# Layer 1's entry in a four-layer graph network: the first norm's statistics taken where z is made, the second norm applied by ScalarE

## The chip, the cores and the metric

The kernel runs on one core of a Trainium2 chip. Its time is the device time of one execution in microseconds (us). Five engines of the core work side by side, each on its own instructions in a fixed order: TensorE (PE, with its weight loads as PEld) multiplies matrices into PSUM, VectorE (DVE) and ScalarE (ACT) work on rows, GpSimd (POOL) does small side work here, and SyncE (SP) issues the loads and stores (DMAs). An instruction waits until what it reads is there, and those behind it on its engine wait with it. All data are 32-bit floats.

## The reference, cut to what matters

Four layers on 3327 nodes with 256 features each, all of the form `x = x + layer(relu(layernorm(x)))`. The change concerns the seam between layer 0 and layer 1:

```python
# layer 0, in two steps n: A is an attention with the smallest probabilities cut off, R the normalised adjacency
Xf = R @ Xf ; Xa = A @ Xa ; Z = Z + Xf @ U1[n].T + Xa @ U2[n].T
h = X + Z                                        # "z" below
x = x + (h - mean(h)) / sqrt(var(h) + 1e-5) * ln_g + ln_b      # the first norm
# layer 1's entry
h = maximum(layernorm(x), 0)                     # the second norm
h2 = tanh(h @ W_proj + b_proj)
gw = h2 @ W_gcn
# layer 1's products
feat = relu(filtered_adj @ gw + b_gcn) ; x = x + feat
```

So for each node row z is normalised, scaled and added to x, and the new x is normalised once more before two small products. Layers 2 and 3 are graph attentions and are not touched.

## The kernel before, in words

The 3327 rows are padded to 26 tiles of 128 rows, and a tile of rows has the nodes on the partitions. The function layer0 (inside layers) holds layer 0 and layer 1's entry.

Step 2 of layer 0 goes over the tiles in groups of three; the last group, the ninth, has two (tiles 24 and 25). For a group, the function group makes logits (line 1037), moves them out of PSUM (1011), takes exponentials (1020), and searches for the threshold of each row in four rounds. A round counts mass with long passes over 3328 columns, on ScalarE (1121, two passes per tile) or on VectorE (1126), and ends in a chain of some 14 VectorE operations on one or two columns (1132 to 1153). After the last round each tile has three more long VectorE passes (1168, 1171, 1182). Then the generator weighted transposes the tile's weights through PSUM (950, 952), multiplies them with the features (940), transposes two rows of results (785, 786), multiplies by U1 and U2 (970) and adds the base row: line 978 makes zrow, a buffer of one, which line 979 stores to zz_d in DRAM. The generator neighbours runs the other product (914) beside it.

Layer 1's entry is the generator entered, in turns divided by yield. Turn 1 loads the row of x (1263) and z back from DRAM (1267) and calls norm_of on z: bn_stats and bn_aggr on VectorE (131, 132) and two one-column GpSimd operations (792, 793: add epsilon, power of minus one half). Turn 2 applies the first norm on VectorE in two passes (1270, 1271) and calls norm_of on the new x. Turn 3 applies the second norm on VectorE (scaled_by, 797), transposes on TensorE (785) and copies out of PSUM with a relu on ScalarE (786). Turns 4 and 5 are the two products (1280, 1285 and 1291, 1294). The buffers of z form a ring of six, inside the slot called kt, which layer 1 uses later for pos_first (1490).

The order of the work comes from two places. The function overlapped steps all running generators once per tick: entries start one per tick, in the last group's rounds (tile it at tick 160 + 12 + it, tiles 24 and 25 at tick 208), and within a tick the older entries come first and the groups last. Then a scheduler that works when the program is built turns this sequence into one fixed order for each engine: an instruction that it finds ready may go ahead of an earlier one that it finds waiting. The trace shows such moves: line 1271 of tile 0 runs after a pass of line 1126 that the sequence has before it, and the loads of x run in two blocks of 13 and 14.

After the entries come weights for layers 2 and 3 (1329 to 1335), and layer 1: per tile of rows it loads a block of the transposed adjacency (1469), filters it (1472, 1473) and multiplies it with gw (1476), while adjacency rows (1488) are turned into masks (1490) and stored (1494). Layer 2's entry (the class Entry) already has the form in which ScalarE applies the norm: its stats adds a third GpSimd operation that forms minus mean times scale (1388), and tile_in has one activation with that bias and scale (1394).

Of the kernel before, what the change touches and what calls it, by code (L numbers as in the profile page):

```python
# [9 lines left out]
F32 = mybir.dt.float32  # L10
# [4 lines left out]
AF = mybir.ActivationFunctionType  # L15
# [5 lines left out]
P = 128  # L21
# [45 lines left out]
def kernel(  # L67
# [678 lines left out]
    def layers(fast):  # L746
# [34 lines left out]
        def transposed(src, dst, relu=False):  # L781

            ps = ps_row()
            for c in range(2):
                nc.tensor.transpose(ps[:, c * P : (c + 1) * P], src[:, c * P : (c + 1) * P], ident)
            nc.scalar.activation(dst, ps[:, :D], AF.Relu if relu else AF.Copy)

        def norm_of(src, pool, name):

            mv = pool.tile([P, 2], F32, tag=name, bufs=3, name=name)  # L790
            stats_of(mv, src)
            nc.gpsimd.tensor_scalar(mv[:, 1:2], mv[:, 1:2], EPS, None, ALU.add)
            nc.gpsimd.tensor_tensor(mv[:, 1:2], mv[:, 1:2], minus_half, ALU.pow)  # L793
            return mv

        def scaled_by(dst, src, mv):
            nc.vector.tensor_scalar(dst, src, mv[:, 0:1], mv[:, 1:2], ALU.subtract, ALU.mult)


        def layer0(wp, mp, ap_, tp, sp):  # L800
# [125 lines left out]
            def weighted(s, it, e, norm, xa, xa_next, us):  # L926

                if s == 0:
                    base = h(it)[:, :D]
                else:  # L930
                    base = tp.tile([P, D], F32, tag="base", bufs=1, name="base_row")
                    nc.sync.dma_start(base, zz_d[it * P : (it + 1) * P, :])
                xf_in = tp.tile([P, D], F32, tag="xf_in", name="xf_in")
                nc.sync.dma_start(xf_in, (xf_d, xf2_d)[s][it * P : (it + 1) * P, :])
                po = ps_out0()[:, :D]

                def products(wt, j0, m):
                    for k in range(m):
                        jc = j0 + k
                        nc.tensor.matmul(  # L940
                            po, wt[:, k * P : (k + 1) * P], xa(jc)[:, :D], start=(jc == 0), stop=(jc == NT - 1)
                        )

                ready = None
                for j0 in range(0, NT, 8):
                    m = min(8, NT - j0)
                    pt = ps_wide()
                    for k in range(m):
                        jc = j0 + k
                        nc.tensor.transpose(pt[:, k * P : (k + 1) * P], e[:, jc * P : (jc + 1) * P], ident)  # L950
                    wt = tp.tile([P, 8 * P], F32, tag="wt", name="wt")
                    nc.scalar.copy(wt[:, : m * P], pt[:, : m * P])  # L952
                    if ready:
                        products(*ready)
                    ready = wt, j0, m
                    yield
                products(*ready)
                if s == 0:
                    row = xa_next(it)[:, :D]
                else:  # L960
                    row = tp.tile([P, D], F32, tag="xa_row", bufs=1, name="xa_row")
                nc.scalar.mul(row, po, norm)
                yield
                xt = turned(row, "xt", 2)
                xft = turned(xf_in, "xft", 2)
                yield
                pz = ps_row()
                for n, (lhs, u) in enumerate(((xft, us[0]), (xt, us[1]))):
                    for cc in range(2):
                        nc.tensor.matmul(  # L970
                            pz[:, :D], lhs[:, cc, :], u[:, cc, :],
                            start=(n == 0 and cc == 0), stop=(n == 1 and cc == 1),
                        )
                if s == 0:
                    keys_of(xt, 1, it)
                yield
                zrow = tp.tile([P, D], F32, tag="zrow", bufs=1, name="zrow")
                nc.vector.tensor_tensor(zrow, pz[:, :D], base, ALU.add)
                nc.sync.dma_start(zz_d[it * P : (it + 1) * P, :], zrow)
                yield  # L980
                if s == 0:

                    xb = tp.tile([P, D], F32, tag="xa_row", bufs=1, name="xb")
                    r = rows_of(it)
                    for a, b in rows_to_load(it):
                        nc.sync.dma_start(xb[a:b], x[it * P + a : it * P + b])
                    nc.gpsimd.tensor_tensor(xb[:r], xb[:r], b_b[:r], ALU.add)
                    nc.sync.dma_start(xb_d[it * P : it * P + r, :], xb[:r])


            b_b = tp.tile([P, D], F32, tag="base", bufs=1, name="b_b")
            nc.sync.dma_start(b_b, bass.AP(tensor=ln_b.tensor, offset=ln_b.offset, ap=[[0, P], [1, D]]))
# [267 lines left out]
            def entered(it):  # L1260
                wps, wgs, g_b, bp, xs_, gw_, temps = places()
                for a, b in rows_to_load(it):
                    nc.sync.dma_start(xs_(it)[a:b], xb_d[it * P + a : it * P + b])

                hz, ht = temps[:, it % 6], temps[:, 6 + it % 2]
                h2 = hz
                nc.sync.dma_start(hz, zz_d[it * P : (it + 1) * P, :])
                mv = norm_of(hz, sp, "mv_z")
                yield
                nc.vector.scalar_tensor_tensor(hz, hz, mv[:, 0:1], g_b, ALU.subtract, ALU.mult)  # L1270
                nc.vector.scalar_tensor_tensor(xs_(it), hz, mv[:, 1:2], xs_(it), ALU.mult, ALU.add)
                mv = norm_of(xs_(it), sp, "mv_1")
                yield
                scaled_by(hz, xs_(it), mv)
                transposed(hz, ht, relu=True)
                yield
                ps = ps_row()
                for m in range(2):
                    for c in range(2):
                        nc.tensor.matmul(  # L1280
                            ps[:, m * P : (m + 1) * P], wps[:, c, m * P : (m + 1) * P],
                            ht[:, c * P : (c + 1) * P], start=(c == 0), stop=(c == 1),
                        )
                for m in range(2):
                    nc.scalar.activation(
                        h2[:, m * P : (m + 1) * P], ps[:, m * P : (m + 1) * P], AF.Tanh, bias=bp[:, m : m + 1]
                    )
                yield
                ps = ps_acc()
                for c in range(2):  # L1290
                    nc.tensor.matmul(
                        ps[:, :D], h2[:, c * P : (c + 1) * P], wgs[:, c, :], start=(c == 0), stop=(c == 1)
                    )
                nc.scalar.copy(gw_(it), ps[:, :D])
                yield
# [433 lines left out]
```

## Time and profile before

| | us |
|---|---|
| median of three runs (lowest, highest) | 3117.26 (3114.98, 3118.21) |
| profiled execution | 3111.67 |
| its span, first to last instruction | 3109.9 |
| PE, DVE, ACT, POOL busy in the span | 2831.8, 2382.5, 1968.2, 375.5 |
| step 2 of layer 0, until the last group's logits | 1065 to 1813 |
| entries of layer 1 (lines 1267 to 1294) | 1814.8 to 2018.9 |
| layer 1's products | 1998 to 2352 |

Stretches are counted in us from the start of the span. Busy time is the time in which an engine ran instructions of the program; matmuls are pipelined and their ends are modelled, so a busy PE is near its limit but not proven to be at it. A wait is put down to the instruction that released it. "Idle before" an instruction is time in which its engine stood still. The view of the chain that ended last follows from the last instruction back to what released each step.

### The profile page before, as it was taken

The numbers are of one execution on the slowest core, as the hardware profiler recorded it, in microseconds if no ns is written. First come the engines' busy times: TensorE is split into PE (matmuls) and PEld (weight loads), VectorE is DVE, ScalarE is ACT, GpSimd is POOL, SyncE is SP. The second block draws the span as 40 slices with busy tenths as digits, with TensorE's granted clock in tenths as the row PEclk, the third lists the DMA queues.
The fourth block names the chain that finished last, engine by engine and source line by source line (L and its number), as shares of the span: only waits on it lengthen the run. The fifth ranks groups of instructions, "written<-read, shape, count | busy, mean of one in ns | idle before, by whom it ended". The sixth has DMA issues, their size and how long they took to land. (4 is left out here: it accounts for less than half of the span.)

```text
span 3109.9 us, 37662 instructions
## 1 busy us (share of the span) xinstructions
PE 2831.8 (91%) x13454; PEld 2278.7 (73%) x13454; DVE 2382.5 (77%) x4159; ACT 1968.2 (63%) x2607; POOL 375.5 (12%) x716
## 2 busy tenths in 40 slices
PE   7788899999999899999999988999997999979998
PEld 5466677777778577767777767788876787758887
DVE  3678888778873588888976868577765999769996
ACT  6767787768763666677665645333334776757776
POOL 0220010000001000000000014311120233210000
PEclk9899999999999999999999999999998999989999
DMA  4431112331242232211232232388861211112221
GB/s 137 131 102 51 55 42 77 91 89 49 70 119 88 76 97 60 59 43 51 73 89 79 76 110 75 111 315 313 321 228 33 71 59 57 31 49 78 72 76 38
DMA packets 183034, 298.83 MB, mean 96 GB/s; under 512 B 24700, under 2 KB 137015, under 8 KB 179511
## 3 DMA queue, kind: packets, MB, share of 16 engines
q1 hardware_dynamic: 182838, 296.34, 30.3%
q8 instruction: 108, 1.77, 0.2%
q14 instruction: 88, 0.72, 0.1%
HBM read 251.97 MB, written 44.30 MB: 95 GB/s over the span
## 5 line engine op out<-in xcount | busy, mean ns | idle before, releaser
L1121 ACT ACTIVATE junk_a<-e,minus 128x3328 int8<-128x3328 f32 x208 | 638.7, 3071 | 3.7
L1588 PE MATMUL ps_wide<-wh,places 128*128 128x257 f32 x1872 | 452.5, 384 | 35.9 <-DVE places L1582 34.8
L1588 PEld LDWEIGHTS ps_wide<-wh,places 128*128 128x128 f32 x1872 | 354.4, 192 | 94.5 <-ACT places L1580 16.5
L914 PE MATMUL ps_acc<-h,blk 128*128 128x258 f32 x1352 | 333.6, 399 | 44.5 <-ACT xf_row L922 35.3
L1011 DVE TENSOR_SCALAR_CACHE_REDUCE e<-ps_wide 128x1024 f32<-128x1024 f32 (+1 forms) x176 | 178.4, 1019 | 212.0 <-PE ps_wide L1037 211.5
L914 PEld LDWEIGHTS ps_acc<-h,blk 128*128 128x128 f32 x1352 | 262.1, 199 | 99.9 <-ACT xf_row L922 40.5
L914 PE MATMUL ps_acc<-xf,blk 128*128 128x256 f32 x1352 | 314.0, 384 | 13.0 <-ACT xf_row L922 13.0
L940 PE MATMUL ps_out<-h,wt 128*128 128x256 f32 x1352 | 312.6, 383 | 5.0 <-ACT wt L952 4.9
L940 PE MATMUL ps_out<-xa,wt 128*128 128x256 f32 x1352 | 312.6, 381 | 1.4 <-ACT wt L952 1.4
L1579 ACT ACTIVATE places<-places,sd 128x512 f32<-128x512 f32 (+1 forms) x364 | 246.6, 685 | 105.5 <-PE ps_wide L1588 72.3
L1476 PE MATMUL ps_wide<-gw,blk 128*128 128x256 f32 x1352 | 303.9, 382 | 0.2 <-ACT blk L1473 0.2
L914 PEld LDWEIGHTS ps_acc<-xf,blk 128*128 128x128 f32 x1352 | 254.1, 191 | 63.2 <-ACT xf_row L922 18.5
L1476 PEld LDWEIGHTS ps_wide<-gw,blk 128*128 128x128 f32 x1352 | 257.0, 192 | 35.1 <-ACT blk L1473 0.6
L940 PEld LDWEIGHTS ps_out<-h,wt 128*128 128x128 f32 x1352 | 250.8, 191 | 41.1 <-ACT wt L952 7.0
L940 PEld LDWEIGHTS ps_out<-xa,wt 128*128 128x128 f32 x1352 | 248.3, 190 | 34.9 <-ACT wt L952 3.7
L1126 DVE SCALAR_TENSOR_TENSOR below<-e,v 128x3328 f32<-128x3328 f32 x72 | 265.4, 3687 | 1.8
L1580 ACT ACTIVATE places<-places,d 128x512 f32<-128x512 f32 (+1 forms) x364 | 235.9, 682 | 46.1 <-DVE places L1581 45.7
L1581 DVE TENSOR_TENSOR places<-places,places 128x1024 f32<-128x1024 f32 (+1 forms) x182 | 210.4, 1164 | 67.8 <-ACT places L1579 65.8
L952 ACT COPY wt<-ps_wide 128x1024 f32<-128x1024 f32 x208 | 175.1, 846 | 88.1 <-PE ps_wide L950 87.4
L1037 PE MATMUL ps_wide<-keys,q 64*128 64x512 f32 (+1 forms) x832 | 214.8, 567 | 16.0 <-DVE e L1011 13.1
L1582 DVE SCALAR_TENSOR_TENSOR places<-blk_s,places 128x1024 f32<-128x1024 int8 (+1 forms) x182 | 206.1, 1141 | 2.0
L1020 ACT ACTIVATE e<-e,nm 128x3327 f32<-128x3327 f32 x44 | 134.8, 3064 | 85.3 <-DVE nm L1019 85.2
(274 smaller groups left out, 4314.8 us busy)
## 6 DMA issues: line engine op xcount, KB each, us to landing
blk<-in_adj_t SPq DMA_DIRECT2D x104, 448.0 KB, 3.4
blk<-in_adj_t SPq DMA_DIRECT2D x52, 832.0 KB, 6.8
adj_rows<-in_adj SPq DMA_DIRECT2D x25, 1663.5 KB, 8.1
blk<-in_adj_t SPq DMA_DIRECT2D x104, 384.0 KB, 3.3
blk_s<-sign_d SPq DMA_DIRECT2D x72, 256.0 KB, 2.9
blk_s<-pos_d SPq DMA_DIRECT2D x44, 416.0 KB, 3.6
pos_d<-pos SPq DMA_DIRECT2D x22, 416.0 KB, 2.8
xf_d<-xf_row SPq DMA_DIRECT2D x52, 128.0 KB, 2.4
```

What stands on the lines that cost most here:

```text
L914: nc.tensor.matmul(acc[:, :w], blk[:, j, :], xf(jc)[:, :w], start=(jc == 0), stop=(jc == NT - 1))
L940: nc.tensor.matmul(po, wt[:, k * P : (k + 1) * P], xa(jc)[:, :D], start=(jc == 0), stop=(jc == NT - 1))
L1011: nc.vector.tensor_scalar(e.rearrange("p (f c) -> p f c", f=2)[:, :, c0 : c0 + cw], pl.rearrange("p (f c) -> p f c", f=2)[:, :, :cw], 1.0, ...
L1037: nc.tensor.matmul(pl[:, f * 512 : f * 512 + cw], q[f * DA : (f + 1) * DA, :], kt[f * DA : (f + 1) * DA, s, c0 : c0 + cw], start=True, sto ...
L1121: nc.scalar.activation(junk, es[i], (AF.Relu, AF.Sign)[n], bias=minus[:, 0, i : i + 1], accum_out=(ga, sa)[n][:, 0, i : i + 1],)
L1126: nc.vector.scalar_tensor_tensor(below, es[i], v[:, 3, i : i + 1], es[i], ALU.is_ge, ALU.mult, accum_out=v[:, 1, i : i + 1],)
L1476: nc.tensor.matmul(po, filt[:, j * P : (j + 1) * P], gw(jc), start=(jc == 0), stop=(jc == NT - 1))
L1579: nc.scalar.activation(e1[:, :, q, :], s0, AF.Exp, bias=sd[:, jc + q, 1:2])
L1580: nc.scalar.activation(e2[:, :, q, :], s1, AF.Exp, bias=d2[:, jc + q : jc + q + 1])
L1581: nc.vector.tensor_tensor(e1, e1, e2, ALU.max)
L1582: nc.vector.scalar_tensor_tensor(e1, signs[:, :n, j : j + 2, :], 0.0, e1, ALU.is_gt, ALU.min)
L1588: nc.tensor.matmul(pos_[k], e1[:, k, q, :], wh(jc + q)[:, : D + 1], start=(jc + q == 0), stop=(eye and jc + q == NT - 1),)
```

## The change

The statistics of z are computed in weighted, directly behind the line that makes zrow, for step 2 only, into a tile mv_z that holds mean and scale of all 26 tiles; turn 1 of entered then only issues the two loads, and turn 2 reads mv_z. The second norm is no longer applied by VectorE: GpSimd forms minus mean times scale in place of the mean, and a ScalarE activation computes relu(scale * x + bias) from SBUF into the buffer that is transposed; the copy out of PSUM behind the transposes becomes a plain copy. Nothing else differs.

```diff
-        def norm_of(src, pool, name):
-
-            mv = pool.tile([P, 2], F32, tag=name, bufs=3, name=name)
+        def norm_of(src, pool, name, mv=None):
+
+            if mv is None:
+                mv = pool.tile([P, 2], F32, tag=name, bufs=3, name=name)
             stats_of(mv, src)
...
                 nc.vector.tensor_tensor(zrow, pz[:, :D], base, ALU.add)
                 nc.sync.dma_start(zz_d[it * P : (it + 1) * P, :], zrow)
+                if s == 1:
+                    norm_of(zrow, sp, "mv_z", mv_z[:, it, :])
                 yield
...
+            mv_z = sp.tile([P, NT, 2], F32, bufs=1, name="mv_z")
...
                 nc.sync.dma_start(hz, zz_d[it * P : (it + 1) * P, :])
-                mv = norm_of(hz, sp, "mv_z")
                 yield
+                mv = mv_z[:, it, :]
                 nc.vector.scalar_tensor_tensor(hz, hz, mv[:, 0:1], g_b, ALU.subtract, ALU.mult)
                 nc.vector.scalar_tensor_tensor(xs_(it), hz, mv[:, 1:2], xs_(it), ALU.mult, ALU.add)
                 mv = norm_of(xs_(it), sp, "mv_1")
+                nc.gpsimd.tensor_scalar(mv[:, 0:1], mv[:, 0:1], mv[:, 1:2], -1.0, ALU.mult, ALU.mult)
                 yield
-                scaled_by(hz, xs_(it), mv)
-                transposed(hz, ht, relu=True)
+                nc.scalar.activation(hz, xs_(it), AF.Relu, bias=mv[:, 0:1], scale=mv[:, 1:2])
+                transposed(hz, ht)
                 yield
```

## The prediction

> **What bounds the kernel now.** The page's busy shares come first: PE 91%, DVE 77%, ACT 63%, POOL 12% of a span of 3109.9 us. TensorE bounds the kernel on average, but the changed lines work in one stretch only, so I looked for the place. The instructions of lines 1270 and 1271 run from 1822.9 to 2010.3 us, and those of line 978 for the second step from 1165.1 to 2002.2. The stretch table (columns: stretch, length, then busy us and instruction count of PE, PEld, DVE, ACT, POOL, granted clock, DMA share, GB/s) cuts this in five:
>
> ```profile
> 1065.00:1813.00 748.00, 702.71 (x3408) 550.38 (x3406) 589.74 (x1131) 503.70 (x460) 44.79 (x125) 1.00 0.25 70
> 1825.00:1838.60 13.60, 6.22 (x29) 5.13 (x27) 12.90 (x15) 6.89 (x6) 1.56 (x4) 0.91 0.77 235
> 1838.60:1977.00 138.40, 118.37 (x654) 98.92 (x655) 119.83 (x283) 68.87 (x132) 57.71 (x101) 0.95 0.20 67
> 1977.00:2002.20 25.20, 25.19 (x141) 22.51 (x142) 3.52 (x10) 7.92 (x18) 2.85 (x11) 1.00 0.25 84
> 2002.20:2020.40 18.20, 15.52 (x80) 12.95 (x79) 10.27 (x32) 5.67 (x10) 5.72 (x10) 1.00 0.67 220
> ```
>
> In the body of step 2 (first row) PE is busy 94%, DVE 79%: PE is the bound. In the 138.4 us of entries (third row) DVE is busy 119.8 us; the waits of DVE in that same window are these:
>
> ```profile
> DVE temps L797 <- POOL mv L793: 12.0, 22, 0.8
> DVE xs L1271 <- POOL mv_z L793: 6.1, 12, 0.7
> ```
>
> 119.8 + 18.1 = 137.9 of 138.4 us: DVE has no free time here, and all its waiting is for GpSimd's two short operations of a norm. PE idles 20.0 us of it (138.4 - 118.4). The chain that ended last says the same. One entry's turn, word for word:
>
> ```profile
> 1920.01 0.74 DVE bn_st L131 x2
> 1920.76 0.09 DVE mv L132
> 1920.85 0.08 issue
> 1920.93 0.23 POOL mv L792
> 1921.16 0.07 issue
> 1921.23 0.69 POOL mv L793
> 1921.92 0.21 POOL mv_z L792
> 1922.13 0.07 issue
> 1922.20 0.60 POOL mv_z L793
> 1922.82 0.49 DVE xs L1271
> ```
>
> The reader should see the loop DVE, POOL, POOL, DVE. Line 1271 starts at 1919.28, 1922.82, 1926.17 and 1929.60: 3.44 us per entry, in which DVE works about 2.5 and waits twice 0.46. Between these instructions lie the small operations of the last group's search (L1132, L1133, L1140, ...), one at a time, so the search is stretched too; its last product (line 1182 of tile 25) ends at 1962.5. From 1977 on PE is full (25.19 of 25.20). After 2020.4 layer 1's products are near PE's limit, with one DMA-fed chain beside them (adj_rows, pos, 1490), and start when the entries' buffer is released.
>
> **What the Trainium skill says.** (1) "SBUF — State Buffer", section "Who interferes with whom": a VectorE instruction with two SBUF inputs and a GpSimd instruction that reads SBUF exclude each other for the whole instruction. The trace agrees: a power on one column, 0.57 to 0.61 us as a rule, took 3.80 us beside such a pass:
>
> ```profile
> 1910.88 3.69 DVE L1126 SCALAR_TENSOR_TENSOR below<-e,v 128x3328 f32<-128x3328 f32 x1
> 1911.19 3.80 POOL L793 TENSOR_TENSOR mv<-mv,minus_half 128x1 f32<-128x1 f32 x1
> ```
>
> (2) "Perfetto Trace Analysis", section "Tensor Engine Instruction (MATMUL, LD_WEIGHTS)": ACT, DVE and GpSimd are strict first-in-first-out, so a waiting instruction holds all behind it. The two waits above agree: other DVE work was ready. (3) "ScalarE: Activation LUTs", section "What ACT_TABLE_LOAD costs": 186 ns, 0.833 ns per element and 93 ns per pointer operand, an estimate of 585 ns for 256 columns with both; the same form in layer 2's entry shows 600, so 0.60 us is used:
>
> ```profile
> L1394 ACT ACTIVATE hr<-xs,mv_a x52: 584/600/603, 2039.6 to 2748.5; 128x256 f32<-128x256 f32 x52
> ```
>
> Its section "Table sets: the hidden batching unit" says that relu is in every set; the trace has no table load after the first softmax, so none is added.
>
> **The change part by part.**
> *Statistics of z moved.* At the entry DVE loses one bn_stats (0.41), one bn_aggr (0.17), and the normalising pass of line 797 (0.41): 22.0 us by the groups of this window (8.9 + 4.0 + 9.1). Neighbouring DVE instructions overlap by about 0.08 us (bn_stats starts at 1920.35, the next starts at 1920.67), so 67 of them free about 22.0 - 5 = 17 us. The 18.1 us of waits go as well: line 1270 and 1271 now read values made long before, and nothing on DVE reads mv_1 any more. The pair put behind line 978 comes back as 0.58 us raw, about 0.5 effective; three of these zrows fall in the window (1.5 us). DVE then needs 119.8 - 17 + 1.5 = 104 us of 138.4. It stops being the bound; PE, with 118.4 us of work, is next. So at most 20.0 us is to be had here, and a PE with nothing else to change would have to be fed without a gap.
> *How much of the 20.0 us.* PE's idle in the window that the waits put on DVE is 8.8 us before L785 on an L1174 (most of it, 7.5 us, ending at 1838.7, before the window), 8.3 on L797, 3.9 on a bank held until line 978 ran, 1.7 on L132, the rest issue gaps and ACT. The L797 waits and most of the gaps shrink with the DVE chain; the 3.9 us sit behind long passes of 3.7 us (1168, 1182), which stay. I take 12 us of 20; the ends are 0 and 20.
> *Head of the stretch.* 7.4 us of PE idle at 1825 to 1838.6 are two long DVE passes in front of entry 0's first statistics. They stay: 0.
> *ScalarE's pass.* 26 x 0.60 = 15.6 us added; 22 of them, 13.2 us, in the window, where ACT has 68.9 us of work: 82.1 of 138.4. The copy out of PSUM stays at 0.38 us. Per entry the way from statistics to transposes grows by one GpSimd multiply (0.27, line 1388's row) and 0.19 us of pass, 0.5 us; entries are pipelined, so this is latency and costs nothing except at the last one. What is late if ACT waits: the copies of line 952 behind it, and so PE.
> *GpSimd.* The two operations on mv_z move, one multiply is added: 26 x 0.27 = 7 us on an engine with 80 us free in the window.
> *Body of step 2.* About 21 pairs, 21 x 0.5 = 10.5 us of DVE in 748 us where DVE has 158 us free and PE 45. They wait for nothing but line 978 before them. Cost 0, hidden by PE's products; if that cover were gone, 10.5 us. Their GpSimd operations stand before line 912's add on that queue; it is busy 44.8 of 748 us there, so 0, at most a few of the 3.8 us blocks.
> *DMAs.* None is added. The read of z on SP's queue keeps its place; the first DVE instruction to wait for it is now line 1270, a turn later. SP's queue itself is unaffected.
> *Buffers.* mv_z is kept for all tiles until line 1271 of the last one, 208 bytes per partition for three times 8. A later tile laid over it could start to load only then; w2l's load is issued at 2004.73 now, so this costs between 0 and the 2 to 3 us to that line; I take 0.
> *The last tile.* Its z lands at 2006.55. The pair and the GpSimd detour before line 1271 (9.85 - 6.55 = 3.3 us) shrink to 0.4: -2.9, and +0.5 for the longer second norm. But the first pass of line 1490 (2020.39) stands on DVE behind two loads of ab, 2005.73 and 2013.66 to 2019, whose only stretch by this chain is one 0.76 us wait among line 1335's first four. I count -1; ends 0 and -3.
> *Afterwards.* Layer 1 starts that much sooner and keeps its own length: what is won at 2020 is won at the end.
>
> Sum: -12 - 1 + 0 = -13 us. The profiled execution took 3111.67 us (span 3109.9, 1.8 around it); it would take 3098.7. The median shown, 3117.26, is 5.6 us above that execution: 3104.3, said as 3104.
>
> **Rivals.**
> *PE is fed without a gap:* all 20 us and 3 at the end: 3094. For it: DVE has 34 us to spare. Against: long passes stay where they are.
> *The gain stays hidden:* the order on each engine is fixed when the program is built, and the last group's search, not DVE's sum, sets the end: four rounds of two 3.07 us ACT passes and a chain of some 14 small DVE operations. If DVE's freed time turns into idle before that chain, about 2 us are left, 3115. For it: between 1825 and 1929 a round takes some 26 us, far above its own chain of about 10, so there is room to gain; that speaks against.
> *ScalarE becomes the bound (slower):* the new pass waits on ACT for GpSimd's column, which long two-input DVE passes block for 3.8 us. In layer 2's entry, the same form, ACT waited 59.9 us in 26 cases for line 1388, 2.3 us each. 22 x 2.3 = 50.6 us against 56.3 us free on ACT: nearly all its slack, with line 952's copies and the search's passes behind. It decides once more than 0.6 us per entry reaches PE beyond today's waits (22 x 0.6 = 13); at 1.0 us, 22 - 13 = +9: 3126. Against: there ACT had little else to do, and today's order already makes ACT wait 27.6 us for line 785.
>
> **How the numbers follow.** Forecast 0.48 (3098 to 3110), PE fed throughout 0.15, hidden 0.15, ScalarE the bound 0.22. Faster by over 0.2%, about 6 us and about what a measurement of this kernel can tell, 0.63; within it 0.15; slower 0.22. The range 3089 to 3125 takes in the full 20 us and most of the slower case; the forecast's own range is 3098 to 3110.
>
> **What would show it.** Right: in the stretch of entries, no DVE wait for GpSimd; line 1271 every 2 us or so where it was every 3.44; tile 25's line 1182 ends between 1942 and 1954, not at 1962.5; PE over 90% busy in it; line 1490 starts near 2007. Wrong: ACT waits on mv for tens of us with PE waiting for line 952; or the body of step 2 longer than before; or DVE idle in the stretch with the last search ending no sooner.

## The result, and the profile after

The changed kernel takes 3102.19 us (median of 6 runs, 3098.58 to 3106.23), the kernel before beside it 3116.12 us (6 runs, 3112.79 to 3121.76). The ratio is 0.9949, with a 95% interval of 0.9938 to 0.9961: faster, by 12 to 19 us. The profiled span went from 3109.9 to 3099.1 us.

That is the forecast's size. The traces show that it did not come from where the forecast put it. From here on line numbers are those of the changed kernel unless said otherwise: 793 and 794 are GpSimd's epsilon and power, 1275 and 1276 the two passes of the first norm (1270, 1271 before), 1278 GpSimd's new product, 1280 ScalarE's new pass, 1286 and 1297 the entry's two products with their evictions 1291 and 1300 (1280, 1291, 1285, 1294 before), 1478, 1482, 1492 and 1496 layer 1's filter, product, clearing and mask (1472, 1476, 1486, 1490 before).

Milestones of the two traces, in us from the start of the span:

| | before | after |
|---|---|---|
| last group's search done (last line 1153 of before) | 1929.06 | 1918.00 |
| first norm of the 24th entry | 1977.32 | 1963.19 |
| last zrow | 2002.20 | 2002.89 |
| last copy of an entry's second product | 2018.51 | 2019.06 |
| first mask of layer 1 | 2020.39 | 2018.89 |
| last product of layer 1 | 2351.45 | 2342.87 |
| from there to the end | 758.4 | 756.2 |

The search ends 11 us sooner, the first norms of 24 entries are done 14 us sooner, and yet the last entry leaves at the same time. The gain appears after that: layer 1's products take 324.0 us where they took 331.1.

The stretch table of the changed kernel (length, then busy us and count of PE, PEld, DVE, ACT, POOL, granted clock, DMA share, GB/s): body of step 2, stretch of entries, end of the entries, layer 1.

```profile
1065.00:1813.00 748.00, 702.70 (x3401) 549.97 (x3400) 597.43 (x1171) 503.83 (x460) 84.73 (x165) 0.99 0.25 70
1838.60:1977.00 138.40, 117.71 (x648) 104.68 (x649) 103.51 (x223) 79.47 (x154) 62.58 (x89) 0.89 0.21 70
1977.00:2018.90 41.90, 39.32 (x221) 34.60 (x219) 9.92 (x34) 13.58 (x31) 5.06 (x20) 1.00 0.42 143
2018.90:2343.00 324.10, 311.90 (x1460) 269.32 (x1461) 222.12 (x248) 107.91 (x147) 52.38 (x104) 1.00 0.78 287
```

In the second row VectorE fell from 119.8 to 103.5 busy us, as worked out (104). TensorE did not follow: 648 matmuls in 117.7 us, where before had 654 in 118.4. The waits of ScalarE, VectorE and TensorE in that same window, from three answers on waits (engine, its line, who released it: total us, times, longest):

```profile
ACT temps L1280 <- POOL mv L1278: 36.3, 13, 6.4
...
DVE temps L1275 <- DMA temps<-zz_d: 11.6, 5, 4.2
DVE temps L1275 <- PE ps_row L785: 6.4, 1, 6.4
...
PE ps_acc L1297 <- ACT temps L1291: 16.1, 6, 6.2
PE ps_row L785 <- ACT temps L1280: 10.0, 1, 10.0
```

VectorE waits for GpSimd no more, as forecast. ScalarE does, 36.3 us in this window and 44.7 us from 1840 to 2020, and TensorE waits 26.6 us for ScalarE (2.6 before). The longest of these waits, 10.0 us, began 6.0 us ahead of the window; the other 20.6 us are nearly all of the 20.7 us that TensorE stands still in it. VectorE also has a new wait, 11.6 us for loads of z: SyncE issues such a load once line 1297 has released a buffer of the ring of six. Before, and with part one alone (below), VectorE had no such wait in this window. The chain that ended last of the changed kernel shows one such turn (start, us, what):

```profile
1873.20 0.10 DVE mv L132
1873.30 0.08 issue
1873.38 0.37 POOL mv L793
1873.75 0.07 issue
1873.82 0.58 POOL mv L794
1874.40 0.09 issue
1874.49 3.62 POOL mv L1278
1878.17 0.48 issue
1878.65 0.35 ACT gw L1300
1879.00 0.11 ACT minus L1119
1879.13 3.16 ACT junk_a L1126 x2
1882.30 0.26 ACT temps L1291
1882.60 1.22 PE ps_acc L1297 x2
```

The reader should see where GpSimd's product of one column, a thing of 0.27 us, becomes 3.62 us: it stands beside the search pass of line 1131, which runs on VectorE from 1874.32 for 3.65 us. ScalarE stood 4.56 us before 1280 for it; behind that, in ScalarE's fixed order, comes the search's own 3.07 us pass, and only then the eviction 1291, for which TensorE had been idle for 5.87 us.

And in layer 1. The kernel before, GpSimd, VectorE and ScalarE by time (start, us, engine, line; in brackets the idle time before it and its releaser):

```profile
2276.63 5.48 POOL L793 TENSOR_TENSOR mv_a<-mv_a,minus_half 128x1 f32<-128x1 f32 x1
...
2277.11 2.83 DVE L1486 MEMSET adj_rows<- 128x3328 f32 x1 [0.64 <-DVE blk L1472]
2279.86 3.62 DVE L1472 SCALAR_TENSOR_TENSOR blk<-blk 128x1664 f32<-128x1664 f32 x2
...
2283.65 0.60 ACT L1394 ACTIVATE hr<-xs,mv_a 128x256 f32<-128x256 f32 x1 [10.60 <-POOL pos L1493]
```

ScalarE's 1394 needs the column of GpSimd's product 1388, which follows the power and ends at 2283.61; the view puts the wait down to 1493, GpSimd's next instruction. The changed kernel at the same tile:

```profile
2274.03 2.07 POOL L794 TENSOR_TENSOR mv_a<-mv_a,minus_half 128x1 f32<-128x1 f32 x1
...
2272.01 3.66 DVE L1478 SCALAR_TENSOR_TENSOR blk<-blk 128x1664 f32<-128x1664 f32 x2
2276.31 2.83 DVE L1492 MEMSET adj_rows<- 128x3328 f32 x1 [0.64 <-DVE blk L1478]
...
2276.50 0.60 ACT L1400 ACTIVATE hr<-xs,mv_a 128x256 f32<-128x256 f32 x1 [6.04 <-POOL pos L1499]
```

None of these instructions belongs to the change. Its order on VectorE is another one: before, the clearing stands between the filters, with the power beside it; after, it comes behind both. Products 1092 to 1144 took 20.56 us before and 12.32 after (from start to start), 8.2 of the 8.6 us by which the last product of layer 1 is earlier. Other groups of 52 products differ by up to 2.2 us in either direction and nearly even out.

### The profile page after: what moved, and what is told of

The parts are those of the page before. It is cut to its first block, busy times and chain, and to the rows that moved or that the text cites. A ratio compares the mean times of both kernels' runs of the same rounds, so it can differ in the third digit from the quotient of the medians.

```text
span 3099.1 us, 37681 instructions
## 1 busy us (share of the span) xinstructions
PE 2823.0 (91%) x13454; PEld 2277.8 (73%) x13454; DVE 2370.4 (76%) x4133; ACT 1979.7 (64%) x2633; POOL 417.8 (13%) x742
## 4 chain that ended last, share of the span: by engine, by line
DVE 38%; PE 27%; ACT 16%; issue 8%; DMA 7%; POOL 3%; SPq 0%; ACTq 0%; POOLq 0%; DVEq 0%
ACT junk_a L1126 9%; PE ps_wide L1594 5%; DVE below L1173 4%; PE ps_out L941 4%; PE ps_acc L915 4%; DVE w L1176 4%; PE ps_wide L1482 4%; DVE below L1131 3%; DVE e L1187 3%; DVE places L1601 3%; DVE places L1587 2%; DVE below L1085 2%; DVE places L1588 2%; DMA blk<-in_adj_t 2%; DMA adj_rows<-in_adj 2%
## 5 line engine op out<-in xcount | busy, mean ns | idle before, releaser
L915 PE MATMUL ps_acc<-h,blk 128*128 128x258 f32 x1352 | 333.3, 399 | 46.8 <-ACT xf_row L923 37.1
L915 PE MATMUL ps_acc<-xf,blk 128*128 128x256 f32 x1352 | 312.9, 384 | 14.3 <-ACT xf_row L923 14.2
L1176 DVE MAX8 w<-below 128x8 f32<-128x3328 f32 x52 | 188.3, 3621 | 0.3
```

What stands on the lines that cost most here:

```text
L915: nc.tensor.matmul(acc[:, :w], blk[:, j, :], xf(jc)[:, :w], start=(jc == 0), stop=(jc == NT - 1))
L1176: nc.vector.max(w9[:, i, 1:9], below)
```

## The experiments

Two theories. **A**, the recorded one: VectorE's relief shortens the stretch of entries. **B**: the change's two parts cancel in the stretch, because ScalarE waits for GpSimd, and what is gained is layer 1's own. All results first, each with the kernel before on the same chip; the last three columns are from one profiled execution each: the start of the last copy of an entry (1294 of before), layer 1 from its first mask to its last product, and the rest of the span.

| kernel | median us | ratio to before (95%) | last entry | layer 1 | rest |
|---|---|---|---|---|---|
| before | 3114.2 to 3116.1 | 1 | 2018.51 | 331.1 | 758.4 |
| after | 3102.19 | 0.9949 (0.9938, 0.9961) | 2019.06 | 324.0 | 756.2 |
| after, again | 3101.04 | 0.9956 (0.9942, 0.9969) | 2017.83 | 325.0 | 758.7 |
| part one alone | 3094.61 | 0.9934 (0.9918, 0.9951) | 2007.34 | 326.6 | 757.2 |
| part one, again | 3091.00 | 0.9925 (0.9911, 0.9938) | 2007.79 | 326.4 | 757.2 |
| part two alone | 3115.76 | 1.0002 (0.9990, 1.0013) | 2029.35 | 326.0 | 757.8 |
| after, no wait for the norm | 3090.59 | 0.9912 (0.9894, 0.9931) | 1994.93 | 332.3 | 758.0 |
| after, one more step | 3097.18 | 0.9947 (0.9934, 0.9961) | 2010.23 | 325.5 | 756.4 |
| after, only the power on GpSimd | 3088.07 | 0.9916 (0.9903, 0.9930) | 2005.56 | 327.2 | 757.3 |
| before, other clearing | 3110.14 | 0.9983 (0.9976, 0.9989) | 2020.84 | 326.3 | 758.3 |
| before, layer 2's columns on VectorE | 3136.92 | 1.0072 (1.0056, 1.0088) | 2018.58 | 344.6 | 769.5 |
| part one, one more step | 3089.21 | 0.9920 (0.9907, 0.9934) | 2002.79 | 329.3 | 757.2 |
| the same, other clearing | 3087.68 | 0.9915 (0.9902, 0.9929) | 2000.98 | 326.3 | 757.7 |
| only the power on GpSimd everywhere, other clearing | 3085.17 | 0.9894 (0.9877, 0.9910) | 2007.69 | 333.3 | 748.5 |

### Part one alone: the first norm's statistics move

The changed kernel with the second norm as it was:

```diff
                 mv = norm_of(xs_(it), sp, "mv_1")
-                nc.gpsimd.tensor_scalar(mv[:, 0:1], mv[:, 0:1], mv[:, 1:2], -1.0, ALU.mult, ALU.mult)
                 yield
-                nc.scalar.activation(hz, xs_(it), AF.Relu, bias=mv[:, 0:1], scale=mv[:, 1:2])
-                transposed(hz, ht)
+                scaled_by(hz, xs_(it), mv)
+                transposed(hz, ht, relu=True)
```

> Part one alone: the first norm's statistics move behind zrow's addition, the second norm stays on VectorE. Theory A (the recorded one: VectorE's relief shortens the stretch of the entries): VectorE loses 22 x (0.41 + 0.17) = 13 us less overlap and the 6.1 us of waits of line 1271, keeps 12.6 us of waits of the second norm; the last entry product (line 1294 of the kernel before) ends 6 to 8 us sooner than 2018.5, layer 1's products keep their 331 us: 3108 to 3110. Theory B (the stretch gains nothing, the gain is layer 1's own order): the last entry product stays within 2 us of 2018.5; the time is then 3116 minus what layer 1's products lose below 331 us, between 3106 and 3117, and layer 1's length alone says it.

Measured: 3094.61 us, faster than either theory said, and the last entry 11.2 us sooner than before. So A's mechanism is real: TensorE runs 723 matmuls in the window of entries where before ran 654. Its stretch row:

```profile
1838.60:1977.00 138.40, 125.69 (x723) 111.91 (x724) 110.90 (x247) 72.87 (x142) 39.52 (x66) 0.94 0.20 67
```

and from the answer on VectorE's waits in that window (798 is the second norm's pass, 797 before):

```profile
DVE temps L798 <- POOL mv L794: 14.3, 21, 1.2
```

VectorE still waits 14.3 us for GpSimd here (18.1 before), 3.8 us less, while its work fell by 8.9 us. The gain is therefore mostly the 0.41 + 0.17 us of statistics per entry, not the waits.

### Part two alone: ScalarE's pass

The kernel before with this alone:

```diff
                 mv = norm_of(xs_(it), sp, "mv_1")
+                nc.gpsimd.tensor_scalar(mv[:, 0:1], mv[:, 0:1], mv[:, 1:2], -1.0, ALU.mult, ALU.mult)
                 yield
-                scaled_by(hz, xs_(it), mv)
-                transposed(hz, ht, relu=True)
+                nc.scalar.activation(hz, xs_(it), AF.Relu, bias=mv[:, 0:1], scale=mv[:, 1:2])
+                transposed(hz, ht)
```

> Part two alone: the second norm's pass goes to ScalarE, z's statistics are taken at the entry as before. Theory A: VectorE loses 9.5 us of passes and 12.6 us of waits in the stretch, the last entry product ends 6 to 8 us sooner than 2018.5: 3108 to 3110. Theory B: ScalarE waits 40 to 70 us for GpSimd's column, TensorE waits for ScalarE's eviction of the entries as in the changed kernel, the last entry product ends at 2018 to 2022; the time follows layer 1's length.

Measured: 3115.76 us, a time that can't be told from that of before; the last entry at 2029.35, 10.8 us later than before. B said 2018 to 2022, so it had the sign right and the size too small. Layer 1's first mask comes 8.8 us later and the layer is 5 us shorter, as in other kernels whose order was planned anew; the profiled span is 3.1 us longer than before. ScalarE's wait in the window of entries (1273 is GpSimd's product and 1275 ScalarE's pass here), and GpSimd's three operations of the second norm:

```profile
ACT temps L1275 <- POOL mv L1273: 35.7, 14, 6.2
...
L793 POOL TENSOR_TENSOR mv<-mv,minus_half 128x1 f32<-128x1 f32 x21 | 18.3, 873 | 1.8
L792 POOL TENSOR_SCALAR mv<-mv 128x1 f32<-128x1 f32 x21 | 16.6, 790 | 61.8 <-DVE mv L132 31.0 <-DVE mv_z L132 11.3 <-DVE a L1148 5.0
...
L1273 POOL TENSOR_SCALAR mv<-mv 128x1 f32<-128x1 f32 x21 | 7.2, 342 | 2.0
```

The new product takes 0.34 us on average here (the number behind the busy time, in ns), not far from 0.27, and ScalarE waits as long as in the change: what it waits for is the whole chain of three.

In the stretch the parts add up: -11.2 and +10.8 alone, +0.6 together.

### The change without the wait

```diff
-                nc.scalar.activation(hz, xs_(it), AF.Relu, bias=mv[:, 0:1], scale=mv[:, 1:2])
+                nc.scalar.activation(hz, xs_(it), AF.Relu, bias=mv_z[:, it, 0:1], scale=mv_z[:, it, 1:2])
```

> The changed kernel, but ScalarE's pass takes its scale and bias from z's statistics, made long before, in place of the second norm's (so the second norm is left out of the result; its statistics and GpSimd's three operations are still done). ScalarE then does not wait for GpSimd in the entry. Theory A: ScalarE's waits for GpSimd cost nothing: within 2 us of the changed kernel, last entry product at 2018 to 2020. Theory B: they cost what VectorE's relief gave: the last entry product ends 6 to 12 us sooner, at 2007 to 2013, and the time is 3091 to 3097 if layer 1 keeps the changed kernel's 324 us.

Measured: 3090.59 us; the last entry at 1994.93, 24 us sooner than in the changed kernel, with the same instructions on every engine, and twice the most that B said. A is out for the second part: ScalarE's waits are no slack. From 1840 to 2020 ScalarE waits 11.4 us for VectorE's line 1276 in place of 44.7 us for GpSimd. The stretch row:

```profile
1838.60:1977.00 138.40, 133.15 (x764) 117.71 (x765) 107.83 (x231) 86.04 (x172) 77.71 (x92) 0.95 0.24 79
```

and what TensorE still waits for in it:

```profile
PE ps_row L785 <- ACT temps L1280: 4.5, 2, 3.5
PE ps_acc L1297 <- ACT temps L1291: 2.6, 5, 1.4
PE ps_row L1286 <- ACT temps L786: 0.9, 2, 0.5
```

The waits for ScalarE fall from 26.6 to 8.0 us. Of the 24 us some 9 (spans) to 12 (medians) reach the end. The rest is given back in layer 1: its first mask comes 19 us sooner, not 24; five tiles in, products wait for a load of adj_rows; and the slow tile is back, 17.77 us for products 1092 to 1144, with the power again beside the clearing:

```profile
2260.06 5.47 POOL L794 TENSOR_TENSOR mv_a<-mv_a,minus_half 128x1 f32<-128x1 f32 x1
...
2260.53 2.83 DVE L1492 MEMSET adj_rows<- 128x3328 f32 x1 [0.64 <-DVE blk L1478]
```

So that loss belongs to neither kernel's entry: it comes and goes with the order that the planner gives VectorE.

### Part one and the whole change on one chip

> The changed kernel once more, beside part one alone on the same chip. Theory B: 5 to 10 us slower than part one alone, 3099 to 3104, last entry product at 2016 to 2021. Theory A: no slower than part one alone. It is also a second look at whether ScalarE's waits for GpSimd in the stretch (44.7 us in the first trace) come back as they were.

> Part one alone once more, for the comparison with the whole change on one chip. Theory B: 3092 to 3097, last entry product at 2005 to 2010. Theory A: the same as the whole change or slower, 3099 to 3105.

3101.04 and 3091.00 us; the intervals of the ratios, 0.9942 to 0.9969 and 0.9911 to 0.9938, do not overlap. Part one is worth 23 us, part two costs 10, by the medians; the spans of the traces, 3109.9 before, 3091.0 and 3092.8 with part one, 3099.1 and 3101.4 with both, show 17 to 19 and 6 to 10. The second trace of the change repeats the first where it matters: last entry at 2017.83, ScalarE's wait 43.7 us (44.7), layer 1 in 325.0 us. The rest of the span is 758.7 us as before, so the 2 us that the first trace showed after layer 1 were no part of the change.

### One more step ahead of ScalarE's pass

```diff
-                mv = norm_of(xs_(it), sp, "mv_1")
+                mv = sp.tile([P, 2], F32, tag="mv_1", bufs=4, name="mv_1")
+                norm_of(xs_(it), sp, "mv_1", mv)
                 nc.gpsimd.tensor_scalar(mv[:, 0:1], mv[:, 0:1], mv[:, 1:2], -1.0, ALU.mult, ALU.mult)
                 yield
+                yield
```

> The changed kernel with one more step between the second norm's columns on GpSimd and ScalarE's pass that reads them (one more buffer for the columns); the computation is whole. Theory B (ScalarE's wait for GpSimd's column eats VectorE's relief): ScalarE waits under 15 us for GpSimd in place of 44.7, the last entry product ends at 1995 to 2004 in place of 2019, the time is 3086 to 3094. Theory A (the waits are slack, something else holds the end of the stretch): it stays within 3 us of 2019, 3098 to 3104.

Measured: 3097.18 us, last entry at 2010.23. The direction is B's, the size is not: ScalarE still waits 29.9 us in the window of entries (35.8 in the second trace of the change). One more step in the program did not take the wait away. By time alone this kernel can't be told from the change, since the two intervals overlap.

### Only the power on GpSimd

```diff
-                mv = norm_of(xs_(it), sp, "mv_1")
-                nc.gpsimd.tensor_scalar(mv[:, 0:1], mv[:, 0:1], mv[:, 1:2], -1.0, ALU.mult, ALU.mult)
+                mv = sp.tile([P, 2], F32, tag="mv_1", bufs=3, name="mv_1")
+                stats_of(mv, xs_(it))
+                nc.vector.tensor_scalar(mv[:, 1:2], mv[:, 1:2], EPS, None, ALU.add)
+                nc.gpsimd.tensor_tensor(mv[:, 1:2], mv[:, 1:2], minus_half, ALU.pow)
+                nc.vector.tensor_scalar(mv[:, 0:1], mv[:, 0:1], -1.0, None, ALU.mult)
                 yield
+                nc.scalar.mul(mv[:, 0:1], mv[:, 0:1], mv[:, 1:2])
```

> The changed kernel with only the power of the second norm left on GpSimd: epsilon and the sign go to VectorE (two operations of about 0.16 us), the product to ScalarE ahead of its pass. GpSimd's chain of three operations becomes one, so one chance to stand beside a long VectorE pass in place of three. Theory B: ScalarE's wait for GpSimd in the stretch falls from 44.7 us to 15 to 30, the last entry product ends at 2005 to 2014, the time is 3090 to 3098. Theory A (these waits are slack): within 3 us of 2019 and of the changed kernel, or slower by ScalarE's 26 x 0.2 us.

Measured: 3088.07 us, a little below B's range, last entry at 2005.56. The stretch row of this kernel:

```profile
1838.60:1977.00 138.40, 125.47 (x738) 111.39 (x739) 106.35 (x274) 90.29 (x193) 32.10 (x43) 0.95 0.21 70
```

and in that window ScalarE's wait for GpSimd and what is left of TensorE's waits (this kernel's own lines: 1280 is GpSimd's power, 1283 and 1284 ScalarE's product and pass, 1290 and 1301 the entry's two products, 1295 the first one's eviction):

```profile
ACT mv L1283 <- POOL mv L1280: 15.8, 7, 5.8
...
PE ps_row L785 <- ACT temps L1284: 9.8, 1, 9.8
PE ps_row L1290 <- ACT temps L786: 4.3, 1, 4.3
PE ps_acc L1301 <- ACT temps L1295: 3.7, 4, 1.1
```

ScalarE has more to do than in the change (90.3 against 79.5 us) and waits less than half as long; 738 matmuls pass where 648 did. The same computation as the change, 13 us faster than it on the same chip (3101.04): the price of part two was the chain of three GpSimd operations, not ScalarE's work.

A rival is that each edit also plans the order of the stretch anew, and that the order alone moves the last entry. No run holds the order fixed. But the six traces that have part one and a ScalarE pass line up: ScalarE's waits for GpSimd from 1825 to 2020 were 44.7 and 43.7 us (the change, twice), 38.0 (one more step), 23.1 and 23.1 (only the power on GpSimd, here and everywhere) and 0 (no wait for the norm), and the last entry left at 2019.06, 2017.83, 2010.23, 2005.56, 2007.69 and 1994.93. That makes the wait the likelier cause.

### Layer 1's slow tile: another clearing in the kernel before

```diff
-                if r < P:
-                    nc.vector.memset(ar, 0.0)
...
+                if r < P:
+                    nc.vector.memset(pos, 0)
+                    nc.vector.memset(counts[:, it : it + 1], 0.0)
                 nc.vector.tensor_scalar(
-                    pos[:, :N], ar[:, :N], 0.0, None, ALU.is_gt, ALU.add, accum_out=counts[:, it : it + 1]
+                    pos[:r, :N], ar[:r, :N], 0.0, None, ALU.is_gt, ALU.add, accum_out=counts[:r, it : it + 1]
                 )
```

> The kernel before, but the last tile's adj_rows are not cleared on VectorE (line 1486, 2.83 us); in place of it the one-byte pos tile and one column of counts are cleared and only the rows that exist are filtered. Nothing of the change is in it. Theory C: layer 1 of the kernel before loses 8.2 us in one tile (products 1092 to 1144 take 20.56 us where 12.32 is usual) because GpSimd's power stands beside that clearing and the passes around it for 5.48 us and ScalarE's layer 2 entry waits for it: without the clearing the tile takes 12 to 15 us and the time is 3107 to 3111, with the last entry product still at 2018.5. Theory D: the tile is lost to something else (the load of adj_rows, the passes themselves): 20 us remain there, 3113 to 3118.

Measured: 3110.14 us, with nothing of the change in it. Products 1092 to 1144 take 13.05 us, not 20.56. GpSimd by time, the power in that place:

```profile
2281.81 2.06 POOL L793 TENSOR_TENSOR mv_a<-mv_a,minus_half 128x1 f32<-128x1 f32 x1
```

Theory C holds for the place and for the time, though the last entry leaves 2.3 us later than C said. Of the 7.5 us some is lost elsewhere: two other groups of 52 products took 18.49 and 19.01 us (15.58 and 15.44 before). The edit also orders the layer anew, so it shows that the tile's loss goes when clearing and power part, not that 5 us are the price of the clearing as such.

### Layer 2's columns on VectorE, in the kernel before

```diff
-                mv = norm_of(src, late, "mv_a")
-                nc.gpsimd.tensor_scalar(mv[:, 0:1], mv[:, 0:1], mv[:, 1:2], -1.0, ALU.mult, ALU.mult)
...
+                nc.vector.tensor_scalar(a, mv[:, 1:2], EPS, None, ALU.add)
+                nc.vector.tensor_scalar(y.bitcast(I32), a.bitcast(I32), -0.5, 1597463007.0, ALU.mult, ALU.add)
+                for _ in range(3):
+                    nc.vector.scalar_tensor_tensor(t, y, y, a, ALU.mult, ALU.mult)
+                    nc.vector.tensor_scalar(t, t, -0.5, 1.5, ALU.mult, ALU.add)
+                    nc.vector.tensor_tensor(y, y, t, ALU.mult)
+                nc.vector.tensor_copy(mv[:, 1:2], y)
+                nc.vector.tensor_scalar(mv[:, 0:1], mv[:, 0:1], y, -1.0, ALU.mult, ALU.mult)
```

> The kernel before, with the columns of layer 2's entry (epsilon, power, product) made on VectorE by a bit trick and three Newton steps, 12 small operations of about 0.16 us, in place of three on GpSimd: nothing in layer 1 waits for GpSimd's power. Theory A: layer 1 is TensorE's, nothing gained, up to +3 us for 26 x 1.9 = 50 us more VectorE work: 3116 to 3120. Theory B: the 5 to 9 us that the changed kernel gains between 2262 and 2294 come from a GpSimd power that was held up there; without it layer 1's products take 322 to 326 us in place of 331: 3107 to 3112.

Measured: 3136.92 us, outside both theories. VectorE's work in layer 1 rises from 220.9 to 252.7 us, of 331 to 345, and ScalarE's waits for the filter pass (1484 here, 1472 before) from 94.5 to 141.4 us:

```profile
ACT blk L1485 <- DVE blk L1484: 141.4, 42, 9.2
```

Layer 1 takes 344.6 us, and layers 2 and 3, where the same class is used, 11 us more. Small operations in a layer with 110 us of free VectorE time are not free; most likely the filter passes that feed TensorE stand behind them. In the one place B was near: products 1092 to 1144 took 14.39 us, not 20.56, with no power of GpSimd there. But more was lost in other tiles, so the run gives no price for the power.

### How far it goes

Part one alone, with one more step ahead of VectorE's pass:

```diff
-                mv = norm_of(xs_(it), sp, "mv_1")
+                mv = sp.tile([P, 2], F32, tag="mv_1", bufs=4, name="mv_1")
+                norm_of(xs_(it), sp, "mv_1", mv)
                 yield
+                yield
                 scaled_by(hz, xs_(it), mv)
```

> Part one alone (the first norm's statistics moved) with one more step between the second norm's columns and VectorE's pass that reads them. In part one alone VectorE waits 16.0 us for GpSimd in 22 cases. Theory E: VectorE is still what bounds the stretch, so these waits count: the last entry product ends at 1994 to 2001 in place of 2007.3, the time is 3082 to 3090. Theory F: TensorE and the transfers bound the stretch by now: within 3 us of 2007.3 and 3092 to 3097.

3089.21 us, last entry at 2002.79, between E and F by place and E by time. VectorE's wait for GpSimd, counted from 1815 to 2000, is 10.0 us, after 16.0 in part one: with that the last entry leaves 4.6 us sooner, of which layer 1, 2.7 us longer in this order, gives part back.

The next kernel adds the other clearing to this one:

```diff
-                if r < P:
-                    nc.vector.memset(ar, 0.0)
...
+                if r < P:
+                    nc.vector.memset(pos, 0)
+                    nc.vector.memset(counts[:, it : it + 1], 0.0)
...
```

> Part one with one more step ahead of the second norm's pass, and the last tile's clearing replaced as in the kernel before without its clearing. In part one with one more step the tile at products 1092 to 1144 already takes 12.32 us. Theory C (the clearing costs only where the power stands beside it): nothing more to gain there, 3086 to 3092. If the clearing costs by itself (2.83 us of VectorE in a stretch where transfers and VectorE feed TensorE): 3083 to 3087.

3087.68 us, in C's range, but only 0.7 us above the other one, and the interval overlaps that of the kernel without this edit. So nothing is seen of a gain, and a cost of the clearing's own of up to its 2.83 us is not ruled out.

The last kernel leaves only the power on GpSimd in every entry, layer 1's and those of layers 2 and 3, with the same clearing. In stats and tile_in of the class Entry, as in layer 1's entry above:

```diff
-                mv = norm_of(src, late, "mv_a")
-                nc.gpsimd.tensor_scalar(mv[:, 0:1], mv[:, 0:1], mv[:, 1:2], -1.0, ALU.mult, ALU.mult)
+                mv = late.tile([P, 2], F32, tag="mv_a", bufs=3, name="mv_a")
+                stats_of(mv, src)
+                nc.vector.tensor_scalar(mv[:, 1:2], mv[:, 1:2], EPS, None, ALU.add)
+                nc.gpsimd.tensor_tensor(mv[:, 1:2], mv[:, 1:2], minus_half, ALU.pow)
+                nc.vector.tensor_scalar(mv[:, 0:1], mv[:, 0:1], -1.0, None, ALU.mult)
...
+                nc.scalar.mul(mv[:, 0:1], mv[:, 0:1], mv[:, 1:2])
```

> The changed kernel with only the power left on GpSimd, in layer 1's entry and in the entries of layers 2 and 3 (epsilon and sign on VectorE, product on ScalarE), and with the last tile's clearing replaced by the one-byte one. Theory C, carried further: layer 1's products lose time only where ScalarE's layer 2 entry waits for GpSimd; they take 318 to 322 us from the first pos filter in place of 327 with only the first entry's chain shortened, and the time is 3080 to 3086. If those waits are slack apart from the one place beside the clearing: 3085 to 3090, with the two small operations per tile on VectorE costing up to 3 us.

3085.17 us, the lowest median here (0.9894; the interval lies below that of the change but overlaps those of several others), and not for the reason given: layer 1 took 333.3 us, not 318 to 322, with one group of 52 products at 18.93 us near its end, while the rest of the span fell from 757.3 to 748.5. Which of the two edits that it adds to the kernel with only the power on GpSimd moved which part, and whether that one group is lost every time, stays open.

## Why the prediction was right, and where it was not

The time was right, 3104 against 3102, and that was luck: the 12 us that I expected from the stretch of entries did not come, and layer 1, where I expected nothing, gave 6 to 7. By its own steps:

- *Statistics of z moved*: right. VectorE's work in the window was put at 104 us and measured 103.5; its waits for GpSimd went; the search ended 11 us sooner. Alone this part brought 11.2 us in the stretch, near the 12 that I took for the whole, though it leaves VectorE the pass of the second norm and 14.3 us of waits. One reading was loose: 3.44 us per entry was one short run of entries; over the stretch they came every 6.4 us before (1829.11 to 1977.32 for 23) and every 5.7 after, where I expected about 2.
- *How much of the 20.0 us*: wrong, and here the sum fails. I took 12; the whole change got 0 (117.7 us of TensorE's work in the window, after 118.4). I priced VectorE's waits that go and set the new wait at nothing.
- *ScalarE's pass, "this is latency and costs nothing"*: the step that failed. ScalarE takes its instructions in order, so its 44.7 us of waiting for the column held up what stood behind: the entry's own evictions 1291, with a 3.07 us search pass between, and TensorE with them. Free time on GpSimd (80 us) and on ScalarE (56 us) was no cover.
- *GpSimd, 26 x 0.27*: too low. The window's groups of the second norm's operations in the changed kernel say what they cost beside the search's long passes:

```profile
L1278 POOL TENSOR_SCALAR mv<-mv 128x1 f32<-128x1 f32 x24 | 22.5, 936 | 2.3
L794 POOL TENSOR_TENSOR mv<-mv,minus_half 128x1 f32<-128x1 f32 x24 | 21.0, 875 | 1.7
L793 POOL TENSOR_SCALAR mv<-mv 128x1 f32<-128x1 f32 x24 | 11.4, 476 | 31.1 <-DVE w L1178 14.9 <-ACT temps L786 9.2 <-DVE bad L1659 4.1
```

  The product takes 0.94 us on average, not 0.27, and the three together 2.29, where 0.22 + 0.57 + 0.27 = 1.06 is their price with no pass beside them. I had quoted the exclusion and a power of 3.80 us beside a pass, and used the free price all the same. But the product's price alone did not decide: in part two alone it was 0.34 us, the three took 2.01, and the last entry was 10.8 us late.
- *What is late if ACT waits*: I named the copies of line 952 of before; it was the entry's evictions and its transposes.
- *The rival that ScalarE becomes the bound*: its mechanism is what happened to part two. It was priced at 22 x 2.3 = 50.6 us of waits, and 44.7 were measured; its point of decision was 13 us reaching TensorE beyond the waits of before, and part two costs 10.8 us (2029.35 less 2018.51) to 11.7 (2019.06 less 2007.34) in the stretch. So the stretch came out level, not slower: of the case that I gave 0.22 the mechanism came, the loss did not.
- *Afterwards, "Layer 1 starts that much sooner and keeps its own length"*: wrong in both halves. It starts 1.5 to 2.7 us sooner (two traces) and is 6 to 7 us shorter. Every edit to the entry made the planner order layer 1 anew; in most of those orders the clearing and the power no longer stand side by side. In the kernel before, and in the change without its wait, they do.
- *Body of step 2*: right at this resolution. VectorE's 7.7 us more (597.4 after 589.7) are hidden behind TensorE's 702.7 us, the same as before. GpSimd's busy time rises by 40 us, chiefly since the moved powers took 1.40 us on average there, where 0.57 is usual, but that is hidden too:

```profile
L794 POOL TENSOR_TENSOR mv_z<-mv_z,minus_half 128x1 f32<-128x1 f32 x20 | 28.0, 1400 | 1.7
```

- *The last tile, buffers, DMAs, head of the stretch*: the first mask came 1.5 us sooner in all where 13 were forecast, so the -1 for the last tile can't be read from it. The head did not stay: TensorE's wait there was 10.0 us, ending at 1842.67, where it had been 7.5, ending at 1838.69; with part one alone it was 9.4. Of the DMAs, the loads of z now make VectorE wait 11.6 us, which I had at nothing.
- *What would show it*: no VectorE wait for GpSimd was there. The "wrong" sign, ScalarE waiting tens of us for the norm's column, was there too; TensorE over 90% in the window was not (85%), nor line 1490 of before near 2007 (2018.89). Tile 25's line 1182 of before ended at 1954.8, a little after the 1942 to 1954 of the forecast. Part one alone shows both of the missing signs: 125.7 of 138.4 us is 91%, and its first mask comes at 2007.18.

In short: -11 for part one, +11 for part two, and -6 to -7 in layer 1 from an order that neither part is about. Two things stay open. The traces place 8.5 to 10.8 us (the spans), the medians differ by 13 to 14; what lies between can't be placed from single executions. And the slow tile explains 7 to 8 us of layer 1's length by its place, while the kernel before with another clearing gains only 5 in all, since each new order loses something elsewhere.

## What to carry to other kernels

A wait moved from one engine to another is not removed: price it with what stands behind it in the new engine's order, and price a small GpSimd operation at what it takes beside the passes that will run there, once for each operation of the chain. Test a change of two parts part by part, since one may pay for the other. And where a program's order is planned anew for each edit, look for the gain by milestones before crediting the edit: here most of the gain that the traces place lay 250 us behind the changed lines.

## What was not expected of the hardware

Beside a clearing on VectorE (128 x 3328 floats, 2.83 us) and a pass of 1.8 us behind it, GpSimd's power on one column took 5.48 and 5.47 us in two traces, 0.57 where nothing stood beside it. The Trainium skill, "SBUF — State Buffer", section "Who interferes with whom", counts a VectorE instruction with at most one SBUF input and outside the two-port modes as free of contention and names a memset as contending for another chip only. In these two traces the power, begun 0.47 to 0.48 us ahead of the clearing, ended only when the pass behind it was over. That fits a clearing that blocks GpSimd. Against it, in eight other traces GpSimd's product on one column, begun 0.11 to 0.12 us ahead of the same clearing, ended inside it after its usual 0.26 to 0.27 us. No run here isolates it.

TensorE's granted clock in the stretch was not the same in all kernels: 0.95 before, 0.89 and 0.88 in the two traces of the change, 0.94 and 0.93 in part one, 0.89 in part two alone, 0.95 without the wait. The three traces at 0.88 and 0.89 each show three gaps of over 3.5 us in TensorE's work there, the others one or two; but the change with one more step shows three as well, at 0.94. Whether gaps in TensorE's work lower the clock wasn't tried.
